# Transposing layer-norm rows on VectorE in 32x32 blocks, placed by DMA, instead of on TensorE

## The chip, the cores and the metric

The kernel runs on one NeuronCore of a Trainium2 chip. A core has engines with an instruction stream each: TensorE (PE in the profile, with PEld for its weight loads), VectorE (DVE), ScalarE (ACT), GpSimd (POOL) and SyncE (SP, which here only issues DMAs). They work side by side and wait for each other by semaphores; each takes its own instructions in order. The DMAs run on 16 DMA engines. Data lies in SBUF (128 partitions); TensorE writes to PSUM. The metric is the device time of one execution in microseconds. The kernel before takes 3035.59 us, the median of three runs (3035.33 to 3039.14).

## The reference

Two layers follow each other on x, 4 sequences of 1024 rows with 512 features, all in 32-bit floats.

```python
# layer 0: graph attention over 20 key rows, 16 heads, two directions
self_feat = concat([v, q_exp]) @ W_self.T + b_self
output = self_feat + gat(direction 0) + gat(direction 1)
x = v + relu(output)
# layer 1: a transformer block modulated by the condition c
sh_msa, sc_msa, g_msa, sh_mlp, sc_mlp, g_mlp = split(silu(c) @ W_mod + b_mod, 6)
x = x + g_msa * attention(layernorm(x) * (1 + sc_msa) + sh_msa, W_qkv, W_out, b_out)
x = x + g_mlp * (gelu((layernorm(x) * (1 + sc_mlp) + sh_mlp) @ W1 + b1) @ W2 + b2)
```

Attention has 16 heads of 64 features over 1024 keys; W1 is 512x2048 and W2 2048x512. The change concerns the two modulated layer norms, whose results stand in front of W_qkv and W1.

## The kernel before

Rows are taken in tiles of 128 (32 tiles, 8 for each sequence, called batch here), and for layer 1 in blocks of four tiles (VB = 4, 512 rows). Three stages follow each other.

**Graph attention** (up to about 412 us). A loop over s runs the 32 row tiles through a software pipeline: TensorE multiplies, DVE, ACT and POOL share the softmax. Its end writes x1 to DRAM and takes the row statistics. In its steps 14 to 27 the first two norm blocks (batch 0) are prepared.

**Attention** (412 to about 2270 us). There are 256 steps: 4 batches, 8 pairs of heads, 8 tiles of queries. In a step TensorE makes the scores of two heads ("psc"), DVE takes the row maxima ("mx"), ACT the exponentials ("w"), ACT and POOL scale them, and DVE transposes them in 32x32 blocks into "wd" (`turn`, L1191). Every second step SP issues eight DMAs that place these blocks in "wT" (L1195), and some two steps later TensorE multiplies them with the values ("pav"). "wd" has three buffers, "wT" two. All else is a list named `fill` of pieces with an earliest and a latest step, a cost in units and a place within the step: projections ("q"), output products ("pu"), loads, sums. A small planner chooses the steps of the products by unit costs; pieces with equal earliest and latest step stay where they are put. Place 4 is the end of a step. TensorE works in seven products instead of eight where blocks of 2x2 are multiplied (`seven`, L520), which needs sums of rows and of weights, made by POOL (`row_sum`, L610).

**MLP** (2270 us to the end). For each of 8 norm blocks, four groups of up products (seven each), then a down projection of seven products "a, c, b, a2, b2, d, b3" (32 matmuls each). The function `between` (L1637) stands after the first down product and prepares the next block; DVE and ACT are lightly loaded. One tile hT holds the normed rows for all blocks of the stage, so it can be written only when the up products are done.

**The norm.** `norm_load` (L412) fetches four row tiles into "xl" (SP). `norm_row` (L418) subtracts the mean and scales, in place. `norm_T` (L433) then makes hT, the transposed rows, 128 features on the partitions by 512 rows, for feature group c of four: four TensorE transposes into one PSUM bank, and one instruction of ACT (or DVE) that moves the bank to hT with the features' scale and shift:

```python
for n in range(VB):
    nc.tensor.transpose(
        pt[:, n * P : (n + 1) * P], xl[st, k * VB + n][:, c * P : (c + 1) * P], ident
    )
...
    nc.scalar.activation(hT[st, k][:, c, :], pt, AF.Identity, scale=scale, bias=shift)
```

Where these stand: in the graph-attention stage one c in each of the steps 17 to 20 and 24 to 27. In the attention stage, before the next batch begins at step `at`, two c in each of the steps at-12, at-11 and at-7, at-6 (L1267 to L1274); the row sums follow at at-7 to at-4 and the first products that read them from at-5. For the first MLP block, steps NS-11 and NS-10, with NS the number of steps (L1328). In the MLP stage all four c stand in `between`, where TensorE's banks "ma" and "mc" are used in turn, and for all blocks but the first every second c goes through DVE.

Of the kernel before, what the change touches and what calls it, by code (L numbers as in the profile page):

```python
# [15 lines left out]
ALU = mybir.AluOpType  # L16
# [25 lines left out]
def cond_block_kernel(  # L42
# [89 lines left out]
    with ExitStack() as gctx:  # L132
# [297 lines left out]
            for i in range(k * VB, (k + 1) * VB):  # L430
                norm_row(st, i, on_act)

        def norm_T(st, k, c, bank, on_act=True):  # L433

            sh, sc = NORM[st][4:]
            b = k * VB // NT
            if st == 1 and k > 0:
                hT[st, k] = hT[st, 0]
            elif c == 0:
                hT[st, k] = rp.tile([P, FC, VB * P], F32, name="hT", tag="hT", bufs=2)  # L440
            pt = bank("ptn")
            for n in range(VB):
                nc.tensor.transpose(
                    pt[:, n * P : (n + 1) * P], xl[st, k * VB + n][:, c * P : (c + 1) * P], ident
                )
            scale, shift = modT[:, sc + c, b : b + 1], modT[:, sh + c, b : b + 1]
            if on_act:
                nc.scalar.activation(hT[st, k][:, c, :], pt, AF.Identity, scale=scale, bias=shift)  # L448
            else:
                nc.vector.tensor_scalar(hT[st, k][:, c, :], pt, scale, shift, ALU.mult, ALU.add)  # L450

        def load_w(held, key, tag, src, cols):

# [176 lines left out]
        def mlp_rows():  # L630

            h = hT[1, 0]
            if "mlp" not in tx:
                tx["mlp"] = xp.tile([P, 6, F], F32, name="tx", tag="tx")
            o = [tx["mlp"][:, k, :].rearrange("p (c r) -> p c r", c=2) for k in range(3)]
            sums_b(nc.gpsimd, o, h[:, :2, :HB], h[:, :2, HB:], h[:, 2:, :HB], h[:, 2:, HB:])
# [221 lines left out]
            if 0 <= i < NTA:  # L858
                f(i)

        def bank_l0(name):
            return ps.tile([P, F], F32, name=name, tag="tr")

        def bank_pf(name):
            return psa.tile([P, F], F32, name=name, tag="pf", bufs=2)

# [7 lines left out]
        for s in range(-4, NTA + 2):  # L874
            do(g_load, s + 4)
            if s >= -2:
                do(g_loadmask, s + 4)
            if s in (1, 7, 13, 23):
                g_modload(s // 6)
            do(g_scores, s)  # L880
            if s == 1:

                do(g_self, s + 2)
            if s == NTA:
                ahead(4)
# [24 lines left out]

            if s in (6, 12, 22, 29):
                g_mod((s - 5) // 6 - s // 29)
            if s == 12:
                rstd(rs1, mv1, nm1, 0, NT)
            if s in (14, 21):
                norm_load(0, s // 7 - 2)
            if 15 <= s - s // 22 * 7 <= 16:
                for i in range(2):
                    norm_row(0, s // 22 * VB + 2 * ((s - 15) % 7) + i)
            if s in (17, 18, 19, 20, 24, 25, 26, 27):  # L920
                norm_T(0, s // 24, (s - 17) % 7, bank_l0)
# [19 lines left out]
    with ExitStack() as actx:  # L941
# [9 lines left out]
        NB = S // QB  # L951
        wout, gate = {}, {}
        vt, oT, xr, wn, wd, wT = {}, {}, {}, {}, {}, {}

        turns = []

        def bank_q(name):

            turns.append(0)
            return (q1, q2)[len(turns) % 2]  # L960


        def load_out(b, g):

# [258 lines left out]
        def add(lo, hi, units, place, f, *args):  # L1223
            fill.append((lo, hi, units, place, lambda: f(*args)))
# [15 lines left out]
        for b in range(B):  # L1240
# [22 lines left out]
            for gp in range(NP):  # L1263
                g, p = divmod(gp, 2)
                at = s0 + gp * NT
                if gp == 0 and b > 0:
                    for h, (ld, rws, tr) in enumerate(  # L1267
                        ((-18, (-15, -14, -14, -13), -12), (-10, (-9, -9, -8, -8), -7))
                    ):
# [279 lines left out]
    with ExitStack() as mctx:  # L1549
# [42 lines left out]
        def new_bank(name):  # L1592

            flip.append(0)
            return up_banks[("ma", "mc")[len(flip) % 2]]

        def short():
            return mp2.tile([P, F], F32, name="s", tag="s", bufs=2)

        flip = []  # L1600
        rows2 = {}
        NB2 = NTA // VB
        for k in range(NB2):
# [32 lines left out]

            def between():  # L1637
                if nxt < NB2:
                    for c in range(FC):
                        norm_T(1, nxt, c, new_bank, on_act=(k == 0 or c % 2 == 1))  # L1640
                if k * VB % NT == 0:
                    spread(2, b, gate2)
                    spread(3, b, bias2)
                for n in range(VB):
                    i = k * VB + n
                    rows2[n] = rp.tile([P, F], F32, name="x2", tag="xl", bufs=VB)
                    nc.sync.dma_start(rows2[n], x2d[i])
                if nxt < NB2:
                    mlp_rows()
# [73 lines left out]
```

## Time and profile before

One execution was taken by the profiler: its span from the first to the last instruction is 3034.2 us, 1.4 us less than the median of the three runs (3035.59); a time of its own for that execution, outside the span, is not given.

| what | value |
|---|---|
| median of three runs | 3035.59 us |
| span of the profiled execution | 3034.2 us |
| PE busy in the span | 2999.3 us (99%) |
| DVE / ACT / POOL busy | 1999.6 / 1432.0 / 1339.4 us |
| attention stage, 412 to 2270 us: PE / DVE busy, DMA share | 1842.62 / 1485.13 us, 0.75 |
| MLP stage, 2270 to 3034 us: PE / DVE / ACT busy, DMA share | 755.90 / 213.27 / 159.53 us, 0.11 |
| norm transposes on PE | 256 of 128x128, 0.272 us each, overlapping |
| modulation from PSUM, ACT / DVE | 0.777 / 0.810 us each |
| granted TensorE clock | 1.000 |

Busy time of PE counts overlapping matmuls once and its ends are modelled, so a PE that is busy for 99% is not necessarily what every step waits for; the chain of waits and the gaps between products tell more. The DMA share is the mean busy share of the 16 DMA engines. A row of the group views gives line, engine, operation, output and input tile, count, and the duration as minimum, median and maximum in ns.

### The profile page before, as it was taken

Reading aid. Unit: us, or ns where it says so; the run is one execution under the profiler, and the core shown is the slowest. Engines: PE = TensorE matmul, PEld = TensorE weight load, DVE = VectorE, ACT = ScalarE, POOL = GpSimd, SP = SyncE. Lnnn points to the kernel's source line nnn. Section 1 sums busy time; section 2 is a strip of 40 time slices with the busy share of each in tenths; the row PEclk is TensorE's granted clock in tenths of the full one; section 3 lists DMA queues with packets and bytes.
Section 4 is the critical chain, followed back from the end, with each engine's and each line's share of the span. In section 5 each row is a group of like instructions: output and inputs, shape, how many; then the busy total and the mean of one; then the engine's idle time right before and its main releaser. Section 6 shows DMA issues by size and latency. Waiting matters only on the chain.

```text
span 3034.2 us, 41780 instructions
## 1 busy us (share of the span) xinstructions
PE 2999.3 (99%) x15317; PEld 1980.2 (65%) x15317; DVE 1999.6 (66%) x2836; ACT 1432.0 (47%) x2368; POOL 1339.4 (44%) x922
## 2 busy tenths in 40 slices
PE   9999999999999999999999999999999999999999
PEld 6666655555555555555555555555568888888888
DVE  3888867777878877878787878877863222222322
ACT  3344456555755565755555755556641221112211
POOL 1444456555656655656655656655721110111010
PEclk9999999999999999999999999999999999999999
DMA  6433357777868777768777868766871010101110
GB/s 201 140 118 121 117 129 180 162 171 179 192 157 210 181 168 179 192 155 211 187 159 180 191 159 205 189 162 164 203 196 63 14 49 28 49 21 35 35 42 15
DMA packets 282695, 417.90 MB, mean 138 GB/s; under 512 B 28968, under 2 KB 101092, under 8 KB 282492
## 3 DMA queue, kind: packets, MB, share of 16 engines
q1 hardware_dynamic: 282256, 415.03, 53.8%
q8 instruction: 123, 2.02, 0.3%
q14 instruction: 80, 0.66, 0.1%
q10 hardware_dynamic: 236, 0.20, 0.0%
HBM read 120.93 MB, written 25.76 MB: 48 GB/s over the span
## 4 chain that ended last, share of the span: by engine, by line
PE 83%; DVE 7%; ACT 3%; POOL 3%; issue 2%; DMA 2%; SPq 1%; POOLq 0%; DVEq 0%; ACTq 0%
PE q L533 19%; PE psc L1156 15%; PE pav L1064 13%; PE pu L1139 6%; PE mbd L533 5%; PE mbu L533 5%; PE mad L533 4%; PE mau L533 3%; PE mcd L533 2%; PE mdd L533 2%; PE mdu L533 2%; PE mcu L533 2%; DVE mx L1167 1%; ACT w L1173 1%; POOL t L742 1%
## 5 line engine op out<-in xcount | busy, mean ns | idle before, releaser
L1182 POOL TENSOR_SCALAR w<-w,sm 128x1024 f32<-128x1024 f32 x256 | 728.6, 2846 | 701.5 <-DVE sm L1178 686.4
L1173 ACT ACTIVATE w<-psc,mx 128x1024 f32<-128x1024 f32 x512 | 570.7, 1115 | 642.6 <-DVE mx L1167 641.6
L1191 DVE STREAM_TRANSPOSE wd<-w 128x1024 f32<-128x1024 f32 x512 | 632.2, 1235 | 109.3 <-ACT w L1180 96.0
L1167 DVE TENSOR_REDUCE mx<-psc 128x1 f32<-128x1024 f32 x512 | 599.2, 1211 | 80.2 <-PE psc L1156 77.0
L1156 PE MATMUL psc<-kT,qT 64*128 64x512 f32 x2048 | 526.9, 615 | 3.1 <-ACT kT L1024 1.4
L1064 PE MATMUL pav<-wT,v 128*64 128x256 f32 x4096 | 482.1, 383 | 1.2 <-DMA wT<-wd 0.6
L1064 PEld LDWEIGHTS pav<-wT,v 128*64 128x64 f32 x4096 | 296.1, 137 | 224.0 <-issue 86.0
L1156 PEld LDWEIGHTS psc<-kT,qT 64*128 64x128 f32 x2048 | 201.6, 186 | 220.5 <-issue 151.2
L1180 ACT ACTIVATE w<-w,sm 128x1024 f32<-128x1024 f32 x256 | 291.0, 1137 | 0.0
L512 POOL TENSOR_TENSOR tx<-hT 128x512 f32<-128x512 f32 x8 | 10.3, 1288 | 596.5 <-ACT hT L448 596.5
L1148 DVE TENSOR_TENSOR xr<-pu,xr 128x512 f32<-128x512 f32 x210 | 143.5, 683 | 78.9 <-PE pu L1139 78.7
L533 PE MATMUL q<-hT,wqk 128*128 128x512 f32 (+1 forms) x396 | 181.2, 581 | 1.0 <-DVE q L547 1.0
L555 ACT COPY mbu<-mau 128x512 f32<-128x512 f32 x30 | 17.1, 570 | 276.5 <-PE mau L533 276.5
L719 PE MATMUL pa<-kp,sfT 128*128 128x320 f32 x512 | 143.5, 433 | 1.4 <-ACT sfT L694 1.4
L533 PEld LDWEIGHTS q<-hT,wqk 128*128 128x128 f32 x396 | 74.7, 190 | 80.9 <-issue 78.2
L533 PE MATMUL q<-tx,ex 128*128 128x512 f32 (+1 forms) x264 | 123.5, 591 | 1.8 <-POOL tx L618 1.3
L719 PEld LDWEIGHTS pa<-kp,sfT 128*128 128x128 f32 x512 | 94.8, 190 | 38.2 <-ACT sfT L694 1.9
L679 PE MATMUL pf<-wx,xT 128*128 128x512 f32 x256 | 116.0, 596 | 0.0
L533 PE MATMUL mad<-w,hs 128*128 128x256 f32 x512 | 113.1, 379 | 0.0
L533 PEld LDWEIGHTS mad<-w,hs 128*128 128x128 f32 x512 | 97.3, 190 | 13.2
L1139 PE MATMUL pu<-wout,oT 128*128 128x256 f32 x360 | 98.4, 396 | 4.2 <-DVE xr L1148 3.7
L1139 PEld LDWEIGHTS pu<-wout,oT 128*128 128x128 f32 x360 | 62.6, 189 | 59.3 <-issue 31.6
(309 smaller groups left out, 4590.7 us busy)
## 6 DMA issues: line engine op xcount, KB each, us to landing
wT<-wd SPq DMA_DIRECT2D x1024, 256.0 KB
wqk<-in_w_qkv SPq DMA_DIRECT2D x64, 256.0 KB
xT<-in_xt SPq DMA_DIRECT2D x32, 256.0 KB
xs<-in_x SPq DMA_DIRECT2D x32, 256.0 KB
x1d<-xs SPq DMA_DIRECT2D x32, 256.0 KB
xl<-x1d SPq DMA_DIRECT2D x32, 256.0 KB
wv<-in_w_qkv SPq DMA_DIRECT2D x32, 256.0 KB
xr<-x1d SPq DMA_DIRECT2D x32, 256.0 KB
```

Of the source, the lines that this page charges most:

```text
L533: nc.tensor.matmul(t[:, q * width : (q + 1) * width], lhsT=lhs(which, q, k), rhs=rhs(which, q, k), start=(fresh and q == 0 and k == 0), st ...
L679: nc.tensor.matmul(pfs[i], lhsT=xT[i][:, c, :], rhs=wx[:, c, :], start=False, stop=(c == FC - 1), skip_group_check=True,)
L719: nc.tensor.matmul(pas[i][:, n, :HF], lhsT=sfT2[i][:, c, :], rhs=kp[:, b, c, n * HF : (n + 1) * HF], start=False, stop=(c == FC - 1), skip ...
L1064: nc.tensor.matmul(po[j * D : (j + 1) * D, :], lhsT=vt[b, g][:, m, p * P + j * D : p * P + (j + 1) * D], rhs=w[:, j, :, m, :], start=(m == 0),
L1139: nc.tensor.matmul(pu[0][:, q * HB : (q + 1) * HB], lhsT=a[:, q * P : (q + 1) * P], rhs=r, start=(bool(fresh) and q == 0), stop=True, skip ...
L1148: nc.vector.tensor_tensor(o, pu[0].rearrange("p (r f) -> p r f", r=2), o, ALU.add)
L1156: nc.tensor.matmul(sc[j][:, n * F : (n + 1) * F], lhsT=qT[b, gp][q, t * P : (t + 1) * P], rhs=kT[b, gp][q, n * F : (n + 1) * F], start=Tru ...
L1167: nc.vector.tensor_reduce(mx, sc, axis=AX.X, op=ALU.max, negate=True)
L1173: nc.scalar.activation(w, sc, AF.Exp, bias=mx, accum_out=sm)
L1180: nc.scalar.mul(w, w, sm)
L1182: nc.gpsimd.tensor_scalar(w, w, sm, None, ALU.mult)
L1191: nc.vector.transpose(wd[j][:, :, at, :], wn.pop((b, gp, t, j)).rearrange("p (m k) -> p m k", k=U))
```

## The change

DVE now transposes each normed row tile in 32x32 blocks into a spare tile. In such a result a block stands still and only its inside is turned, so four DMAs on SP's queue for each row tile move the blocks to hT, in runs of 32 elements (128 B). A partition of hT then holds other features than before; the host puts the rows of W_qkv and W1, and the columns of W_mod and b_mod for shift and scale, into the same order. ACT applies scale and shift in place on hT.

```diff
+        def norm_turn(st, k, n, home):
+            if st == 1 and k > 0:
+                hT[st, k] = hT[st, 0]
+            elif n == 0:
+                hT[st, k] = rp.tile([P, FC, VB * P], F32, name="hT", tag="hT", bufs=2)
+            t = home(n)
+            nc.vector.transpose(
+                t.rearrange("p (m k) -> p m k", k=RB),
+                xl.pop((st, k * VB + n)).rearrange("p (m k) -> p m k", k=RB),
+            )
+            for u in range(P // RB):
+                at = n * P + u * RB
+                nc.sync.dma_start(hT[st, k][:, :, at : at + RB], t[RB * u : RB * (u + 1), :])
+
+        def norm_mod(st, k, c):
...
+            o = hT[st, k][:, c, :]
...
+            nc.scalar.activation(o, o, AF.Identity, scale=scale, bias=shift)
+
+        def home_blocks(key):
+            def home(n):
+                if key not in blocks:
+                    blocks[key] = xp.tile([P, 6, F], F32, name="tt", tag="tx")
+                return blocks[key][:, n, :]
...
-            if s in (17, 18, 19, 20, 24, 25, 26, 27):
-                norm_T(0, s // 24, (s - 17) % 7, bank_l0)
+            if s in (17, 18, 24, 25):
+                for i in range(2):
+                    norm_turn(0, s // 24, 2 * ((s - 17) % 7) + i, home_blocks(0))
+            if s in (19, 20, 26, 27):
+                for i in range(2):
+                    norm_mod(0, s // 24, 2 * ((s - 19) % 7) + i)
...
-                        ((-18, (-15, -14, -14, -13), -12), (-10, (-9, -9, -8, -8), -7))
+                        ((-18, (-15, -14, -14, -13), (-12, -12, -11, -11), -10), (-10, (-9, -9, -8, -8), (-8, -8, -7, -7), -6))
...
+                        for n, tn in enumerate(tr):
+                            add(at + tn, at + tn, 0, 4, norm_turn, 0, 2 * b + h, n, home_blocks(b))
                         for c in range(FC):
-                            add(at + tr + c // 2, at + tr + c // 2, 0.4, 3, norm_T, 0, 2 * b + h, c, bank_q)
+                            add(at + md, at + md, 0, 4, norm_mod, 0, 2 * b + h, c)
                     for k in range(4):
-                        add(at - 7 + k, at - 7 + k, 0, 4, row_sum, b, k)
+                        add(at - 6 + k, at - 6 + k, 0, 4, row_sum, b, k)
...
+        for n in range(VB):
+            add(NS - 11 + n // 2, NS - 11 + n // 2, 0, 4, norm_turn, 1, 0, n, home_blocks("mlp"))
         for c in range(FC):
-            add(NS - 11 + c // 2, NS - 11 + c // 2, 0.4, 3, norm_T, 1, 0, c, bank_q)
+            add(NS - 9, NS - 9, 0, 4, norm_mod, 1, 0, c)
...
             def between():
                 if nxt < NB2:
-                    for c in range(FC):
-                        norm_T(1, nxt, c, new_bank, on_act=(k == 0 or c % 2 == 1))
+                    for n in range(VB):
+                        norm_turn(1, nxt, n, lambda n: short() if n % 2 else tx["mlp"][:, 5, :])
...
+            def modulated():
+                for c in range(FC):
+                    norm_mod(1, nxt, c)
+                mlp_rows()
...
                 if n == 0:
                     between()
+                if n == 3 and nxt < NB2:
+                    modulated()
```

The tile "tt" takes the place of the row sums "tx" in SBUF before these are made. The transposed rows of a block now stand two tiles to a step in the steps where TensorE's transposes stood or one step earlier, all four modulations of a block in one later step (at-10, at-6, NS-9), and the row sums at at-6 to at-3. In the MLP stage the transposes and their DMAs stand in `between`, with two spare places (the last sixth of "tx" for even tiles and the short buffers for odd ones); modulation and row sums follow after the fourth down product.

More of the change, by code (lines that the diff above doesn't have):

```diff
@@ L431, in norm_rows @@
                 norm_row(st, i, on_act)
-        def norm_T(st, k, c, bank, on_act=True):
+        RB = 32
+        blocks = {}
+        def norm_turn(st, k, n, home):
[12 more added lines that the diff above has]
+        def norm_mod(st, k, c):
             sh, sc = NORM[st][4:]
             b = k * VB // NT
[L437 to L445, printed above, removed]
-            scale, shift = modT[:, sc + c, b : b + 1], modT[:, sh + c, b : b + 1]
[L447 to L450, printed above, removed]
+            o = hT[st, k][:, c, :]
+            scale, shift = modT[:, sc + c, b : b + 1], modT[:, sh + c, b : b + 1]
+            nc.scalar.activation(o, o, AF.Identity, scale=scale, bias=shift)
[4 more added lines that the diff above has]
+                return blocks[key][:, n, :]
+            return home
         def load_w(held, key, tag, src, cols):
@@ L859, in do @@
                 f(i)
-        def bank_l0(name):
-            return ps.tile([P, F], F32, name=name, tag="tr")
         def bank_pf(name):
@@ L953, in cond_block_kernel @@
         vt, oT, xr, wn, wd, wT = {}, {}, {}, {}, {}, {}
[L955 to L960, printed above, removed]
         def load_out(b, g):
@@ L1266, in cond_block_kernel @@
                 if gp == 0 and b > 0:
-                    for h, (ld, rws, tr) in enumerate(
-                        ((-18, (-15, -14, -14, -13), -12), (-10, (-9, -9, -8, -8), -7))
+                    for h, (ld, rws, tr, md) in enumerate(
+                        ((-18, (-15, -14, -14, -13), (-12, -12, -11, -11), -10), (-10, (-9, -9, -8, -8), (-8, -8, -7, -7), -6))
                     ):
@@ L1590, in dn_rhs @@
             return w2s[2 * h + k][:, r, f * HB : (f + 1) * HB]
-        def new_bank(name):
-            flip.append(0)
-            return up_banks[("ma", "mc")[len(flip) % 2]]
         def short():
             return mp2.tile([P, F], F32, name="s", tag="s", bufs=2)
-        flip = []
         rows2 = {}
@@ L1647, in between @@
                     nc.sync.dma_start(rows2[n], x2d[i])
-                if nxt < NB2:
-                    mlp_rows()
                 for n in range(VB):
                     nc.gpsimd.tensor_tensor(rows2[n], rows2[n], bias2, ALU.add)
+            def modulated():
+                for c in range(FC):
+                    norm_mod(1, nxt, c)
+                mlp_rows()
             def dn_done(i, j, t):
@@ L1684, with spread_features @@
     mask = np.asarray(mask_BxSxSx11_ik0)
+    def spread_features(a):
+        n = f // P
+        return a.reshape(n, n, P // n, -1).transpose(1, 2, 0, 3).reshape(a.shape)
+    w_mod, b_mod = np.array(L1_cond_W_mod), np.array(L1_cond_b_mod)
+    for k in (0, 1, 3, 4):
+        cols = slice(k * f, (k + 1) * f)
+        w_mod[:, cols] = spread_features(w_mod[:, cols].T).T
+        b_mod[cols] = spread_features(b_mod[cols])
     adj = np.stack([mask[:, :, :NG, :], mask[:, :NG].transpose(0, 2, 1, 3)])
@@ L1701 @@
         "gbo": L0_cond_bout,
-        "w_mod": L1_cond_W_mod,
-        "b_mod": L1_cond_b_mod,
-        "w_qkv": L1_cond_W_qkv,
+        "w_mod": w_mod,
+        "b_mod": b_mod,
+        "w_qkv": spread_features(np.asarray(L1_cond_W_qkv)),
         "w_out": L1_cond_W_out,
         "b_out": L1_cond_b_out,
-        "w1": L1_cond_W1,
+        "w1": spread_features(np.asarray(L1_cond_W1)),
         "b1": L1_cond_b1,
```

## The prediction

> **What bounds the kernel now.** The page's first part gives PE 2999.3 of 3034.2 us, so I went to stages, then to the places where the change acts. The chain of waits names PE for 83% of the span, and it also shows where PE is not the bound.
>
> The MLP stage first: the timeline around the end of one product of the down projection (start, duration, engine, line, operation).
>
> ```profile
> 2385.76 7.07 PE L533 MATMUL mad<-w,hs 128*128 128x256 f32 x32
> 2392.45 0.57 PEld L443 LDWEIGHTS mcu<-ident,xl 128*128 128x128 f32 x4
> ...
> 2394.17 0.42 PEld L443 LDWEIGHTS mcu<-ident,xl 128*128 128x128 f32 x4 [0.70 <-DVE hT L450]
> ...
> 2394.66 0.63 PE L443 MATMUL mau<-ident,xl 128*128 128x128 f32 x4
> ...
> 2395.13 7.07 PE L533 MATMUL mcd<-w2x,hx 128*128 128x256 f32 x32
> ```
>
> Products follow each other every 6.91 us here except where the norm's sixteen transposes stand: the chain has "mad" from 2385.92 to 2392.83 and "mcd" from 2395.29, a gap of 2.46 us that PE alone pays.
>
> Then the attention stage at a change of batch, with engine time by windows (width, then busy time and count for PE, PEld, DVE, ACT, POOL, then clock, DMA share, GB/s). The old transposes stand at 780, 786, 811 and 817.
>
> ```profile
> 700.00:775.00 75.00, 74.65 (x423) 44.76 (x422) 58.31 (x76) 44.93 (x70) 44.91 (x32) 1.00 0.72 174
> 775.00:781.00 6.00, 6.00 (x38) 3.45 (x37) 5.76 (x8) 4.93 (x8) 2.85 (x1) 1.00 0.34 55
> 781.00:787.00 6.00, 6.00 (x41) 3.59 (x39) 5.53 (x8) 4.92 (x8) 2.85 (x1) 1.00 0.90 201
> 787.00:794.00 7.00, 6.92 (x36) 3.92 (x36) 6.50 (x11) 6.19 (x11) 3.15 (x2) 1.00 0.94 239
> 794.00:800.00 6.00, 5.90 (x34) 3.02 (x34) 5.93 (x8) 2.96 (x6) 5.34 (x5) 1.00 0.91 228
> 800.00:806.00 6.00, 5.81 (x33) 3.04 (x32) 5.39 (x9) 4.01 (x7) 2.84 (x1) 1.00 0.97 272
> 806.00:812.00 6.00, 6.00 (x36) 3.56 (x36) 5.62 (x8) 4.99 (x8) 2.85 (x1) 1.00 0.90 244
> 812.00:818.00 6.00, 6.00 (x39) 4.22 (x38) 5.71 (x8) 5.19 (x9) 5.19 (x3) 1.00 0.76 181
> ```
>
> Here three things are full at once: PE, DVE (40.4 of 43 us from 775 to 818) and the DMA engines (33.2 of the 37 us from 781 to 818). The chain of waits in the same place passes through a load:
>
> ```profile
> 796.90 1.19 PE pav L1064 x9
> 798.09 4.70 DMA xl<-x1d
> 802.79 0.02 issue
> 802.81 1.52 ACT xl L421 x2
> ```
>
> SP's own timeline there is back to back: eight "wT" DMAs from 789.61 for 8.37 us, four "xl" loads (798.09, 3.09 us), eight "wT" DMAs from 801.95 for 8.70 us, one "wout" load; the next pause is 811.3 to 814.75. The change adds DMAs and DVE work at this place.
>
> **The change part by part.** Prices come from these rows.
>
> ```profile
> L1191 DVE STREAM_TRANSPOSE wd<-w x512: 1203/1235/1248, 415.2 to 2232.9; 128x1024 f32<-128x1024 f32 x171
> L421 ACT ACTIVATE xl<-xl,nm,rs x28: 799/805/821, 760.6 to 2156.3; 128x512 f32<-128x512 f32 x28
> L363 SPq DMA_DIRECT2D vb<-vrd x36: 274/337/349, 42.8 to 58.4; - x36
> ```
>
> A norm row tile (128x512) becomes one DVE transpose, half the 1235 ns: 0.62 us; and four SP DMAs, each 64 KB in 512 runs of 128 B. There are 64 row tiles, so 256 new DMAs: 32 in the graph-attention stage, 96 at the three batch changes, 16 for the first MLP block, 112 in the MLP stage. Removed are 256 PE transposes. The modulation stays 64 instructions of 128x512, 12 of them moved from DVE to ACT in the MLP stage, where ACT is busy 160 of 764 us; in place one costs 0.805 (nearest row L421) where it cost 0.777: under 2 us in all, hidden by ACT's idle half.
>
> Price of one new DMA. No SBUF-to-SBUF transfer in 128 B runs exists before. The nearest row in run length is the spread of the "vb" values (128 B runs from DRAM): the DMA view of 56 to 58 us.
>
> ```profile
> q1 hardware_dynamic: 355, 0.04, 12.6%
> ```
>
> That is 0.126 x 16 x 2 us / 355 = 11.4 ns a packet; 32 packets on each of 16 engines give 0.36 us. From above: the "wqk" loads (512 B runs, 341 to 344 us: 1322 packets at 92.8%) take 34 ns a packet, some of them longer runs; the run of 512 such packets would be 1.1 us at most. Between them, "wT" (SBUF to SBUF) takes 1.05 us for 256 KB where the "xl" load takes 0.77: factor 1.36. I take 0.36 x 1.36 = 0.49 us, say 0.5, as the vb row is the nearest in run length; the ends are 0.36 and 1.1. SP's issue of 0.34 lies inside that. The Trainium skill (DMA: Bandwidth & Descriptors, Rules for kernel authors) warns against transposing by a plain DMA with a rearranged access pattern and puts the loss at 19 times. From wT's 0.26 us for 64 KB that would be an estimated 5 us a DMA, some 150 us a batch change, and a time near 3550; the vb row speaks against it, since here each run is 32 elements and not one. The same page (Why small descriptors are slow) says that SBUF-to-SBUF transfers are spared the penalty; then a DMA would be an estimated 0.26 us, the batch changes would cost only DVE's share below, and the sum would be near 3033. No run before shows either.
>
> MLP stage. Seven gaps close: 2.68 (the first, 2293.45 to 2296.13) + 6 x 2.46 = 17.4 us, all on PE. The cover is the down projection, 7 products x 6.91 = 48 us from the first one's start. Inside it must fit: transposes after DVE's sums end (2387.7, while PE is in the first product), the third waiting for the first one's DMAs since they share a slot, sixteen DMAs at 0.5 (8 us, 18 at the upper end) with about 1.6 us landing (798.09 + 4.70 against 3.09 of issue), the four "x" loads queued behind them on SP (2.6), ACT's four modulations (3.2), POOL's sums after its bias adds (8 x 1.27). In series about 27 us from the first product's start, 34 at the upper end. ACT's copy of the "c" product may wait for a short buffer; its reader on PE comes 14 us later. Only if the series passed 48 us would the next up product be late, so I take -17.4; the ends are that and -10, one us kept in each gap by the shared buffers.
>
> Graph-attention stage. PE loses 8 groups of four (weight loads 252.04 to 252.48: 0.43 each), 3.4 us; DVE gains 8 x 0.62 = 5.0, in four steps of about 10 us in which it is busy 8.6 and its softmax instructions carry the chain. Ends -3.4 and +5.0; I take +1, as PE is shown full (10.00 of 10) beside a DVE with 1.4 us free for 1.24 in each. DMA there is at a third.
>
> Attention stage, three batch changes and one MLP block. PE is relieved of 4.15 us a change, 2.08 for the block (windows of those instructions alone). That is worth nothing where DVE and DMA are full too, so 0; if PE alone were the bound, -14.5.
> DVE: 8 x 0.62 = 5.0 a change against 2.6 free. That is +2.4 a change alone, and it would overlap with the next.
> DMA: 32 x 0.5 = 16 us a change into 3.8 free. Behind them on SP wait the "wT" DMAs, for these "pav" on PE and the "wd" ring on DVE, then ACT, whose modulations stand in order before the next exponentials and now need all DMAs of their rows to have landed. The wT DMAs have some slack: issued 801.95 to 810.65, read two steps after their step began (about 814.3), with 1.6 to land: 2 us for PE, about 4 for DVE's ring. I take 3. So 16 - 3.8 - 3 = 9 a change; three are 27. For the MLP block 8 us into 2 free less the slack: 3. Sum +30. Ends: at 0.36 us 11.5 - 6.8 = 5, with a step (6) more of slack nothing, and DVE's 2.4 remains: +8; at 1.1 us 35 - 6.8 = 28 a change and 13: +97.
> Order: four modulations stand in one step (3.2 us) instead of two in each of two, and the row sums come one step (6.2) later while the products that read them keep their places. The first needs 2 x 0.8 + 2 x 1.27 = 4.1 us after ACT gets there, PE is back after about 2 us of scores: +2 a change, 6 in all; ends 0 and 15. Behind the waiting sum on POOL stands the next scaling of the weights (2.85 us), and POOL has some 3 us free in a step. The wait exists today in small ("PE q L533 <- POOL tx L618: 1.3, 2").
>
> Sum against the profiled span: 3034.2 - 17.4 + 1 + 30 + 6 = 3053.8; the median of the runs shown is 1.4 us above that span, so 3055.
>
> **The rivals.** *Queue hidden (faster)*. The new DMAs fit because wT's slack is a step larger than I read, or because packets cost 11 ns or less. For it: SP waits for DVE at L1195 498 us in total, so on average it has room. Against: the pauses are not in these windows. Then -17.4 + 1 + 8 + 0 gives 3027. It decides once a DMA costs under about 0.36 us, where the overflow is inside the slack. *Everything to PE (faster)*. DVE is no bound either and all 35 us of PE (17.4 + 3.4 + 14.5) come through: 3000. Against it, DVE's 40.4 of 43. *Packets dear (slower)*. 0.8 us a DMA: 25.6 - 6.8 = 19 a change, 8 for the block: +65, giving 3090; at 1.1 it is +97, 3122. For it: neither row has short runs on both the reading and the writing SBUF side. *The MLP gain fails*: the waits through the shared slot pass 48 us; +17 to any of these. It needs DMAs above 2 us (16 of them reach 32 us beside the 18 of the rest).
>
> **How the numbers follow.** Likeliest (queue partly in the way, 3036 to 3075): 0.5, forecast 3055. Packets dear (3075 to 3122): 0.17. MLP gain fails too: 0.02. Queue hidden: 0.23, mostly 3015 to 3034. Everything to PE: 0.08. A measurement of this kernel tells about 0.2% (6 us) from no change. Of the hidden queue 0.19 lies below 3029.5 and 0.04 in the band, and 0.03 of the likeliest does: faster 0.27, same 0.07, slower 0.66. The range 3015 to 3095 leaves out about 1 in 10 on each side; the likeliest's own range is 3036 to 3075.
>
> **What would show it.** Right: in the MLP stage products at 6.91 us without gap; around the batch changes DMA share near 1 over some 50 us, SP without pause, waits of "pav" or of DVE's "wd" on "wT", of ACT's modulation on the hT DMAs, and windows that are some 10 us longer; packets of 128 B near 15 ns. Wrong: a batch change as long as before with DMA below 0.95, or an MLP gap that remains before "mcd" or in front of the next up product.

## The result and the profile after

The changed kernel takes 3122.45 us (median of four runs, 3120.5 to 3125.46) against 3036.76 us before on the same chip (3035.33 to 3039.14): 1.0279 times as long, with a 95% interval from 1.0264 to 1.0294. The prediction was 3055 with a range from 3015 to 3095. The direction was right and the size was not: 86 us were lost where 19 were expected, and the time lies outside the range. The profiled execution has a span of 3123.7 us, 89.5 more than before, and a mean granted clock of 0.987 (1.000 before).

Where the 89.5 us lie can be read from where each stage begins, with the first scores as the mark of the attention stage: it begins 12.1 us later than before. Each of the three batch changes then adds 27.9, 25.3 and 25.5 us and the preparation of the first MLP block 15.9. The MLP stage is shorter, 747.0 us against 763.8. That makes 12.1 + 94.6 - 16.8 = 89.9, the span's difference but for reading errors.

The MLP stage, read as before from the timeline around the end of the first down product:

```profile
2392.98 7.07 PE L549 MATMUL mad<-w,hs 128*128 128x256 f32 x32
2399.88 7.07 PE L549 MATMUL mcd<-w2x,hx 128*128 128x256 f32 x32
```

The gap of 2.46 us in front of "mcd" is gone; products follow each other after 6.90 us, as the prediction had it.

A change of batch, by windows (columns as in the windows shown of before):

```profile
805.00:811.00 6.00, 4.92 (x24) 2.67 (x26) 5.93 (x9) 2.76 (x5) 3.57 (x2) 1.00 0.72 96
811.00:817.00 6.00, 2.19 (x14) 1.11 (x10) 1.11 (x2) 2.60 (x4) 2.10 (x3) 0.85 0.82 136
817.00:823.00 6.00, 4.53 (x9) 2.20 (x10) 3.02 (x5) 3.80 (x7) 1.47 (x1) 0.58 0.91 227
...
847.00:853.00 6.00, 0.03 (x2) 0.00 (x0) 2.36 (x2) 2.86 (x5) 5.10 (x6) 0.69 0.85 144
853.00:859.00 6.00, 4.86 (x6) 2.19 (x7) 2.60 (x4) 3.29 (x6) 2.61 (x2) 0.50 0.89 232
```

Before, PE was nearly full in each window here. Now it is busy for only 2.19 of 6 us at 811 to 817 and for 0.03 at 847 to 853, and DVE for 1.11 and 2.36. These are not full engines but waits that stop nearly everything. Behind each the granted clock is low for one window, 0.58 and 0.50. The timeline names what ended the waits (in brackets: idle time before the instruction, and its releaser):

```profile
814.40 2.92 ACT L457 ACTIVATE hT<-hT,modT 128x512 f32<-128x512 f32 x4 [6.63 <-DMA hT<-tt]
818.47 3.85 PE L1165 MATMUL psc<-kT,qT 64*128 64x512 f32 x7 [5.17 <-ACT w L1182]
...
850.14 2.93 ACT L457 ACTIVATE hT<-hT,modT 128x512 f32<-128x512 f32 x4 [4.54 <-DMA hT<-tt]
851.74 2.35 POOL L634 TENSOR_TENSOR tx<-hT 128x1024 f32<-128x1024 f32 x1 [0.82 <-ACT hT L457]
854.14 3.78 PE L549 MATMUL q<-tx,ex 128*128 128x512 f32 x4 [7.12 <-POOL tx L634]
```

In the first case ACT stands in front of its four modulations until the new DMAs have landed; the next exponentials are queued behind them, so DVE and then PE run dry. In the second the wait passes through the modulations to POOL's row sum and then to the first product that reads it. SP's timeline in the same stretch has no pause:

```profile
789.84 8.95 SPq L1204 DMA_DIRECT2D wT<-wd  x8
798.90 1.79 SPq L472 DMA_DIRECT2D wqk<-in_w_qkv  x2
800.80 11.68 SPq L449 DMA_DIRECT2D hT<-tt  x16
812.58 8.39 SPq L1204 DMA_DIRECT2D wT<-wd  x8
821.07 3.38 SPq L415 DMA_DIRECT2D xl<-x1d  x4
824.56 10.54 SPq L1204 DMA_DIRECT2D wT<-wd  x8
...
835.86 12.22 SPq L449 DMA_DIRECT2D hT<-tt  x16
```

The chain of waits there names the queue itself. From 810.39 to 826.91 it follows SP's issue instructions one after the other and goes on to a wT DMA and to DVE, where before it was PE that filled the chain:

```profile
812.58 0.57 SPq L1204
...
825.80 1.11 SPq L1204
...
826.96 4.54 DMA wT<-wd
831.52 1.29 DVE tt L443 x2
```

And the new instructions, from the group views of their lines (count, then minimum, median and maximum in ns):

```profile
L449 SPq DMA_DIRECT2D hT<-tt x144: 609/636/1717, 260.6 to 2277.4; - x144
L443 DVE STREAM_TRANSPOSE tt<-xl x36: 661/683/703, 259.9 to 2260.8; 128x512 f32<-128x512 f32 x36
L457 ACT ACTIVATE hT<-hT,modT x64: 797/799/815, 281.5 to 2990.9; 128x512 f32<-128x512 f32 x64
```

A DMA takes SP 0.64 us to issue (median); the two sixteens above take 11.68 and 12.22 us. Two causes were therefore open: the queue of DMAs, and the new order of row sums and products. In the expectations below, Q stands for the queue, O for the order of the pieces and V for VectorE's added work.

### The profile page after: what moved, and what is told of

It reads as the page before. It is cut to its first block, busy times and chain, and to the rows that moved or that the text cites. A ratio compares the mean times of both kernels' runs of the same rounds, so it can differ in the third digit from the quotient of the medians.

```text
span 3123.7 us, 41795 instructions
## 1 busy us (share of the span) xinstructions
PE 3008.3 (96%) x15061; PEld 1957.5 (63%) x15061; DVE 2035.1 (65%) x2888; ACT 1441.5 (46%) x2380; POOL 1341.0 (43%) x922
## 3 DMA queue, kind: packets, MB, share of 16 engines
q8 instruction: 121, 1.98, 0.3%
## 4 chain that ended last, share of the span: by engine, by line
PE 76%; DVE 8%; DMA 4%; POOL 3%; SPq 3%; issue 3%; ACT 2%; POOLq 0%; ACTq 0%; DVEq 0%
PE q L549 17%; PE psc L1165 14%; PE pav L1073 12%; PE pu L1148 6%; PE mbd L549 5%; PE mbu L549 5%; PE mad L549 4%; PE mau L549 3%; SPq L1204 2%; DVE mx L1176 2%; DMA wT<-wd 2%; PE mdd L549 2%; PE mcd L549 2%; PE mdu L549 2%; PE mcu L549 2%
## 5 line engine op out<-in xcount | busy, mean ns | idle before, releaser
L1165 PE MATMUL psc<-kT,qT 64*128 64x512 f32 x2048 | 546.2, 626 | 32.9 <-ACT w L1182 30.3
L1656 POOL TENSOR_TENSOR x<-x,tx 128x512 f32<-128x512 f32 x32 | 40.0, 1280 | 617.0 <-DMA x<-x2d 617.0
L1187 DVE RECIPROCAL sm<-sm 128x1 f32<-128x1 f32 x512 | 72.3, 141 | 74.3 <-ACT w L1182 51.7
```

Of the source, the lines that this page charges most:

```text
L1165: nc.tensor.matmul(sc[j][:, n * F : (n + 1) * F], lhsT=qT[b, gp][q, t * P : (t + 1) * P], rhs=kT[b, gp][q, n * F : (n + 1) * F], start=Tru ...
```

## The experiments

Apart from the first, each kernel has one time beside one or more of the kernel before. The changed kernel's own times spread over 5 us, so differences of that size are not read as gains or losses.

### The MLP part alone

The kernel before, with the change in the MLP stage only. At the batch changes TensorE still transposes. The first MLP block too, but ScalarE writes its normed rows with the features already in the new order.

```diff
+        def norm_row_spread(n):
+            t = home_blocks("mlp")(n)
+            nc.scalar.activation(
+                t.rearrange("r (c a b) -> r b c a", c=FC, b=FC),
+                xl[1, n].rearrange("r (b c a) -> r b c a", b=FC, c=FC),
...
-            add(NS - 15 + n, NS - 15 + n, 0, 4, norm_row, 1, n, True)
+            add(NS - 12 + n // 2, NS - 12 + n // 2, 0, 4, norm_row_spread, n)
-            add(NS - 11 + c // 2, NS - 11 + c // 2, 0.4, 3, norm_T, 1, 0, c, bank_q)
+            add(NS - 10 + c // 2, NS - 10 + c // 2, 0.4, 3, norm_T, 1, 0, c, bank_q)
```

> The change in the MLP stage alone; the graph-attention stage, the batch changes and the first MLP block keep TensorE's transposes (the first MLP block's rows are normed one to three steps later, out of place, so that the features come in the new order). All theories take the MLP stage's gain as independent of the rest: the stage was 763.8 us before and 747.0 after, so 3020 us, 0.994 of before, with 2 us of doubt for the first MLP block. If the loss at the batch changes had its root in the MLP stage's code, it would stay and the time would be above 3030.

Measured: 3020.41 us (median of four, 3019.73 to 3022.49) against 3038.38 before in the same comparison (seven runs, 3035.39 to 3048.14): ratio 0.9934, interval 0.9913 to 0.9955. That is a small gain, 0.7%, but clear of the noise, as expected, and it beats both kernels. The span is 3020.5 us, 13.7 less than before's; the attention stage ends 2.5 us later than there and the MLP stage is 16 us shorter.

```profile
2386.87 7.07 PE L578 MATMUL mad<-w,hs 128*128 128x256 f32 x32
2393.78 7.07 PE L578 MATMUL mcd<-w2x,hx 128*128 128x256 f32 x32
```

Here too "mcd" follows 6.91 us after "mad". So the gain of the MLP stage is real, and the whole loss lies in the two stages ahead of it.

### The DMAs alone, added to the kernel before

Nothing of the change is made; the kernel before issues the DMAs of the batch changes and of the first MLP block in addition, from a tile that is there into a spare one that nobody reads.

```diff
+        def more(key, n):
+            if key not in extra:
+                extra[key] = xp.tile([P, 6, F], F32, name="tt", tag="tx")
+            for u in range(4):
+                at = n * P + u * 32
+                o = extra[key][:, :FC, at : at + 32]
+                nc.sync.dma_start(o, gates[32 * u : 32 * (u + 1), :])
...
+                            e = (-12, -12, -11, -11)[n] if h == 0 else (-9, -9, -8, -8)[n]
+                            add(at + e, at + e, 0, 4, more, b, n)
...
+            add(NS - 11 + n // 2, NS - 11 + n // 2, 0, 4, more, "mlp", n)
```

> The kernel before, with the DMAs of the batch changes and of the first MLP block added and nothing else: 16 of 64 KB in 128 B runs a block, from a constant tile to a spare one, 112 in all, that nothing reads. Theory Q (the DMAs hold up SP's queue, and what stands behind them is late): the wT DMAs are some 10 us late at each change, +8 to +12 us for each of three and +4 for the block, 3065 to 3077. Theory A (the loss is ACT waiting for the landing of what it modulates, in front of its exponentials): nobody waits here, below +10, 3037 to 3047. Theory V (DVE and the later order): no change, 3037.

Measured: 3103.82 us, 65 more than before and above every expected range. Some 20.5, 18.6 and 17.5 us are lost at the three changes and 10 at the block. SP's timeline of this kernel at the first change, and its chief waits there (total us, times, longest):

```profile
789.93 11.14 SPq L461 DMA_DIRECT2D tt<-gates  x16
801.17 8.54 SPq L1206 DMA_DIRECT2D wT<-wd  x8
809.81 3.35 SPq L415 DMA_DIRECT2D xl<-x1d  x4
813.22 7.26 SPq L461 DMA_DIRECT2D tt<-gates  x8
...
830.52 6.41 SPq L461 DMA_DIRECT2D tt<-gates  x8
```

```profile
DVE wd L1202 <- DMA wT<-wd: 15.5, 3, 9.7
...
ACT xl L421 <- DMA xl<-x1d: 14.0, 2, 13.1
```

The DMAs take SP 11.1 + 7.3 + 6.4 = 24.8 us at a change. What waits is what stands behind them in the queue: ACT for its rows, DVE's ring for the wT DMAs. The queue alone can cost most of what the change costs, though nobody reads what these DMAs bring. Two differences from the change remain: the second block's DMAs stand one step earlier here, and the spare tile takes the place of the row sums, which waited 2.5 us for these DMAs in the whole run.

### Longer runs, and fewer DMAs

Two variants of the same addition: the same number and size with runs of 2 KB instead of 128 B, and a quarter of the number (28 of 256 KB) with runs of 128 B.

```diff
-                o = extra[key][:, :FC, at : at + 32]
+                o = extra[key][32 * u : 32 * (u + 1), n, :]
```

> As the kernel with added short runs, but each of the 112 DMAs writes its 64 KB in 32 runs of 2 KB. Theory Q with a price for each run: SP issues one in about 0.35 us instead of 0.63, some 3 us a change, 3040 to 3052. Theory Q with a price for each DMA or byte: as with short runs, 3065 to 3077. Theories A and V: no change, 3037.

```diff
-            for u in range(4):
...
+            o = extra[key].rearrange("p a f -> p (a f)")[:, 768 * n : 768 * n + 768]
+            nc.sync.dma_start(
+                o.rearrange("p (r k) -> p r k", k=48)[:, :, :32], gates.rearrange("p (r k) -> p r k", k=32)
+            )
```

> The same bytes in the same 128 B runs as the kernel with added short runs, but four DMAs of 256 KB (2048 runs) a block instead of sixteen of 64 KB. If SP's time is a price for each DMA: four times 0.63 us, little is late, 3037 to 3048. If it is a price for each run, in issue or in the DMA engines: four times 2.5 us, as with sixteen, 3065 to 3077.

Measured: 3100.98 us with long runs and 3094.14 us with wide DMAs, 63 and 56 more than before. The issue row of the three, in the order short, long, wide (one kernel each):

```profile
L461 SPq DMA_DIRECT2D tt<-gates x112: 623/639/1767, 789.9 to 2244.1; - x112
```

```profile
L461 SPq DMA_DIRECT2D tt<-gates x112: 507/588/1692, 789.4 to 2241.3; - x112
```

```profile
L459 SPq DMA_DIRECT2D tt<-gates x28: 633/1764/4861, 790.4 to 2229.0; - x28
```

Runs sixteen times as long shorten the issue only from 639 to 588 ns, so with 64 KB each the length of the runs is not what SP pays for. A quarter of the number was expected to cost little, and that was wrong: one of 256 KB takes 1764 ns where four take 4 x 639 = 2556. Here the DMA engines are full as well; their share for SP's queue over 788 to 806 us reads

```profile
q1 hardware_dynamic: 10314, 3.40, 102.7%
```

(packets, MB, share of 16 engines; it is 78.0% with the 64 KB DMAs and 67.5% with the long runs). The wT DMAs behind them get slower in turn, 10.12 us for eight where they took 8.54 beside the short ones. Neither shape takes the cost away.

### The change without its DMAs at the batch changes and the first MLP block

```diff
-            t = home(n)
+            change = k > 1 if st == 0 else k == 0
+            t = hT[st, k][:, n, :] if change else home(n)
...
-            for u in range(P // RB):
+            for u in range(0 if change else P // RB):
```

> The changed kernel, but at the three batch changes and for the first MLP block DVE's transposes write straight into hT and the 112 DMAs that place them are left out, so attention and the first MLP block work on wrongly placed rows; the order of modulation and row sums, the graph-attention stage and the rest of the MLP stage stay as changed. Theory Q (SP's queue is held up by these DMAs, and the rest follows from it): the batch changes lose only DVE's and the order's part, 2 to 5 us each instead of 27, so 3122 - 80 = 3036 to 3050. Theory V (DVE's 0.68 us a tile and the later modulation and row sums): most of the loss stays, above 3090.

Measured: 3077.40 us, span 3075.2, between the two theories. The attention stage now loses 48.8 us instead of 94.6, so the DMAs are worth 45.8 in the changed kernel: 10.7, 11.3 and 9.2 at the changes and 14.6 at the MLP block. The other 48.8 us are lost with no new DMA there, 17.2, 14.0 and 16.3 at the changes and 1.3 at the block. Neither cause has it all. POOL's timeline, and the product that waits:

```profile
833.18 2.84 POOL L1192 TENSOR_SCALAR w<-w,sm 128x1024 f32<-128x1024 f32 x1 [1.79 <-PE pu L1149]
835.99 0.73 POOL L529 TENSOR_TENSOR wsum<-wout 128x256 f32<-128x256 f32 x1
...
838.84 2.35 POOL L635 TENSOR_TENSOR tx<-hT 128x1024 f32<-128x1024 f32 x1
...
841.24 3.78 PE L550 MATMUL q<-tx,ex 128*128 128x512 f32 x4 [6.25 <-POOL tx L635]
```

PE waits 6.25 us for the first row sum. Ahead of that sum POOL has no idle time from 833.18 on: a scaling of the weights and four sums of output weights stand before it in its order.

### The order alone, on the kernel before

One line of the kernel before is changed, so that the row sums come one step later; its DMAs, transposes and engines stay as they are.

```diff
-                        add(at - 7 + k, at - 7 + k, 0, 4, row_sum, b, k)
+                        add(at - 6 + k, at - 6 + k, 0, 4, row_sum, b, k)
```

> The kernel before with one number changed: the row sums of each batch at at-6 to at-3 instead of at-7 to at-4, as the change has them. Theory O (with the sums one step later, POOL makes the first of them behind its weight scaling and the sums of the output weights, and TensorE's first product at at-5 waits for it, which alone costs some 9 us, and the second some 4): 25 to 45 us in all, 3062 to 3083. Rival: the wait comes from the four modulations in one step or from DVE's extra work, and not from the place of the sums: below 10 us, 3037 to 3047.

Measured: 3074.54 us against 3036.74, 38 more: 13.4, 13.1 and 12.0 at the three changes. Its products that wait (timeline, PE only):

```profile
825.74 3.37 PE L533 MATMUL q<-tx,ex 128*128 128x512 f32 x4 [3.42 <-POOL tx L618]
...
858.83 3.78 PE L533 MATMUL q<-tx,wqk 128*128 128x512 f32 x4 [5.03 <-POOL tx L618]
```

In the kernel before the same two instructions of the first case read

```profile
818.12 2.36 POOL L618 TENSOR_TENSOR tx<-hT 128x1024 f32<-128x1024 f32 x1
```

```profile
820.75 1.95 PE L533 MATMUL q<-tx,ex 128*128 128x512 f32 x4 [0.49 <-ACT hT L448]
```

The sum ended at 820.48 and the product began at 820.75: 0.27 us of slack. (The 0.49 us in brackets ends with ACT's move of hT, which happened to end later than the sum, at 820.61.) A sum that is made a step later must stop PE. There are two such places at each change: the products of place at-5 need the first sum, and those some three steps later the last one, which in the new order stands behind eight sums of weights on POOL. At the first change the scores fall back by 4.3 us at the first of these products and by 7.0 at the second; another 2 us are lost some 14 us ahead of the first and were not followed up. A part of it goes with the clock: the two products take 3.37 and 3.78 us, at granted clocks of 0.58 and 0.50, where they took 1.95 and 1.98 before. With no DMA and no DVE work added, the place of the sums alone costs 38 us.

### Can the order's loss be taken back?

The products are moved with the sums, one step later, once in the changed kernel and once in the one without DMAs.

```diff
-            ("qk", 0, -5, -5), ("v", 0, -1, 0), ("qk", 1, 2, 3), ("qk", 2, 6, 11), ("v", 1, 9, 16), ("qk", 3, 14, 19),
+            ("qk", 0, -4, -4), ("v", 0, -1, 0), ("qk", 1, 2, 4), ("qk", 2, 6, 11), ("v", 1, 9, 16), ("qk", 3, 14, 19),
```

> The changed kernel with the first products of each batch one step later too, at at-4 instead of at-5, so that the sums have their old lead again (the planner then also places some output products elsewhere). Theory O: 8 to 14 us a change come back, 3080 to 3100. Rival (the late DMA queue alone decides when the sums can be made): 0 to 4 us a change, 3110 to 3122.

> The kernel without the batch changes' DMAs (wrongly placed rows as there), with the first products one step later. What is left at the batch changes is DVE's extra work and the four modulations in one step. Theory O: 8 to 14 us a change below the 3077 of the one without DMAs, 3035 to 3053. Theory V (DVE): most of the 16 us a change stay, 3065 to 3077.

Measured: in the changed kernel 3122.44 us, nothing gained. Without the DMAs 3056.63, 21 less than the 3077.40 with the products in their old places. Two of these lie in the graph-attention stage, so some 6.5 a change come back, fewer than expected; what remains, read in the middle of each batch, is 11, 8 and 9 us a change. In the changed kernel the product no longer waits, but PE stops elsewhere, for exponentials that stand behind the modulations:

```profile
818.06 4.87 PE L1165 MATMUL psc<-kT,qT 64*128 64x512 f32 x8 [6.71 <-ACT w L1182]
```

So the two causes lie over one another: while the queue is late, a better order gains nothing, and alone they cost 38 and 65 us on the kernel before, where together, with DVE's work and the later modulations, they cost 94.6. The remainder of 8 to 11 us a change was not split further. It holds DVE's eight transposes (8 x 0.68 = 5.5 us a change into 2.6 free), the four modulations in one step, and shifts of other products that the planner made.

### Later modulations, another queue, a warm TensorE

Three variants of the changed kernel. The modulations of the first block two steps later:

```diff
-((-18, (-15, -14, -14, -13), (-12, -12, -11, -11), -10), (-10, (-9, -9, -8, -8), (-8, -8, -7, -7), -6))
+((-18, (-15, -14, -14, -13), (-12, -12, -11, -11), -8), (-10, (-9, -9, -8, -8), (-8, -8, -7, -7), -6))
```

> The changed kernel with the modulation of the first block of each batch change at at-8 instead of at-10, one line. Theory A (ACT waits for the hT DMAs in front of its exponentials, 6.6 us at the first change, and TensorE with it): that wait and the slow clock behind it go, 6 to 10 us a change, 3092 to 3104. Theory Q, with everything behind the late queue anyway: ACT will then wait for the late xl loads or DVE for wT instead, 0 to 3 us a change, 3113 to 3122.

The 112 DMAs of the batch changes and the first MLP block on POOL's queue instead of SP's:

```diff
+                e = nc.gpsimd if (k > 1 if st == 0 else k == 0) else nc.sync
+                e.dma_start(hT[st, k][:, :, at : at + RB], t[RB * u : RB * (u + 1), :])
```

> The changed kernel with the 112 DMAs of the batch changes and of the first MLP block issued by POOL instead of SP: the same bytes, runs and DMA engines. If the price is SP's issue and the place in SP's queue: wT is no longer behind them, 10 us or more a change come back, 3075 to 3095, unless POOL's own issue delays its scaling of the weights. If the price is the DMA engines' time: 3115 to 3130. POOL has some 3 us free in a step; if it needs more than 0.4 us for a DMA, it is slower than 3122.

Extra matmuls into a bank that nobody reads, to fill PE's waits:

```diff
+        def warm_up(n):
+            for _ in range(n):
+                nc.tensor.matmul(q1, lhsT=ident, rhs=gates, start=True, stop=True)
+        add(NS - 9, NS - 9, 0, 5, warm_up, 14)
+        for b in range(1, B):
+            at = b * NP * NT
+            add(at - 9, at - 9, 0, 5, warm_up, 12)
+            add(at - 5, at - 5, 0, 0.4, warm_up, 14)
```

> The changed kernel with matmuls that nobody reads put where TensorE waits: 12 of 128x512 (5.2 us) at the end of step at-9, 14 (6.0 us) ahead of the first product at at-5 and at the end of step NS-9. In the changed kernel the granted clock is at half for 82 us around the batch changes and the first MLP block. If the half clock costs time of its own, it goes to 1.0 there and 10 to 30 us come back: 3092 to 3112. If TensorE waits anyway while its clock is low, nothing comes back: 3117 to 3130, and more where a matmul that nobody reads delays the next scores.

Measured: 3120.39, 3143.12 and 3132.84 us, beside 3122.45 for the change as it is. Later modulations give back 2 us, which is within the spread: ACT no longer waits for the hT DMAs of the first block, but stops all the same for the rows that are loaded behind them:

```profile
ACT xl L421 <- DMA xl<-x1d: 12.5, 2, 11.7
```

On POOL's queue each DMA occupies POOL for 747 ns, and it becomes the engine that is late, both for the DMAs and for the row sums (waits of 775 to 880 us):

```profile
ACT hT L458 <- DMA hT<-tt: 22.3, 2, 11.6
...
PE q L550 <- POOL tx L635: 14.2, 1, 14.2
```

With PE kept busy the granted clock is 0.998 instead of 0.987 and the time 10 us longer. This does not settle what the half clock costs, because the added matmuls took more than was meant (PE's timeline at the first change):

```profile
809.67 10.46 PE L1345 MATMUL q<-gates,ident 128*128 128x512 f32 x24
...
844.47 12.28 PE L1345 MATMUL q<-gates,ident 128*128 128x512 f32 x28
```

Each is two instructions, so they hold PE for 10.46 and 12.28 us, twice the 5.2 and 6.0 that the expectation put down, and longer than the waits of 5 to 7 us that they were to fill. A gain by the full clock and a loss by real work that stands behind them can cover each other here. The kernel with the late sums shows that the half clock costs something: the two products behind its waits are 3.2 us longer together, of 13.4 lost at the first change.

### The graph-attention stage: six loads two steps later

In the change the last eight DMAs of this stage and six weight loads are issued in the step in which the next rows are loaded. Here the weight loads come two steps later.

```diff
-            if s == 25:
+            if s == 27:
                 load_qk(0, 0)
```

> The changed kernel with the six loads of the first attention weights issued two steps later in the graph-attention stage (s = 27 instead of 25), so that the loads of x in the next step no longer stand behind eight hT DMAs and these six. If ACT's wait for x, in front of its other work, makes the stage's loss of 9 to 12 us: the attention stage starts 4 us or less later than before, not 9 to 12, and the whole is 3110 to 3118. If DVE's transposes make it: no change, 3118 to 3124.

Measured: the attention stage begins 3.2 us later than before instead of 12.1 (8.4 to 11.3 in six other runs of the same code). The wait of ACT for its rows (330 to 420 us), in the change and then in this kernel:

```profile
ACT xs L175 <- DMA xs<-in_x: 9.2, 2, 7.5
```

```profile
ACT xs L175 <- DMA xs<-in_x: 3.1, 2, 1.9
```

So most of the loss of this stage was a load that stood behind others on SP. The time is 3118.53 us, and the span 6.9 us shorter than the change's (3116.8): the changes and the block read 27.3, 27.1, 26.6 and 15.8, together 2.2 more than there, which takes back a part of the 8.9.

## Why the prediction was wrong

| term | predicted, us | measured, us | from |
|---|---|---|---|
| MLP stage | -17.4 | -16.8 | stage times; -15.8 with the MLP part alone |
| graph-attention stage | +1 | +12.1 | start of the attention stage |
| DMAs and DVE at three changes | +27 | DMAs +31.2 | change against no DMAs |
| DMAs at the first MLP block | +3 | +14.6 | change against no DMAs |
| order at three changes | +6 | +47.5 with DVE's work; the sums' place alone +38 | no DMAs against before |
| the rest at the MLP block | 0 | +1.3 | no DMAs against before |
| sum | +19.6 | +89.9 | |

The split between DMAs and order depends on which is added first: on the kernel before, the DMAs of the changes alone cost 57 us and those of the block 10.

**The failed step is "Order".** It said "+2 a change, 6 in all; ends 0 and 15". The place of the sums alone costs 38, beyond its upper end. The step counted ACT's modulations and two row sums from the moment ACT gets there, and took PE to be busy with scores for about 2 us of that. It did not look at what else POOL had queued ahead of the sum, though it named the scaling that stands behind. And it took a small total of waiting ("1.3, 2") for slack: the sum ended 0.27 us before the product began. By the prediction's own figure a step is 6.2 us, and the sums were moved by one: most of a step had to be paid, and at two places of each change (4.3 and 7.0 us at the first change), where the step counted one of 2 us.

**The MLP term was right**, and so was its cover: 48 us of down products hid transposes, DMAs, modulations and sums.

**The DMA term at the changes, 31.2 for 27, was right in size by luck.** 0.5 us a DMA was taken from the time of the packets. The trace has 14.6 ns a packet, near the 15.5 worked out, but SP's issue is 0.64 us, nearly twice the 0.34 of the "vb" row (DMAs of 10 KB at most), which was put inside the 0.5. With the 24.8 us that the issue takes at a change, the same formula gives 24.8 - 3.8 - 3 = 18, and the DMAs alone on the kernel before cost 17.5 to 20.5, twice the 9 that was forecast. In the changed kernel they add only 9 to 11, because they and the order's waits cover each other in part. The Trainium skill (DMA: Bandwidth & Descriptors) gave two estimates: 5 us a DMA by the 19 times of its Rules for kernel authors, and 0.26 by Why small descriptors are slow, which spares such transfers. Neither fits this case: the packets of a DMA take 0.47 us on 16 engines and its issue 0.64. The 19 times compares with the hardware's DMA transpose, which no run here has. The same page (Issuing engines are not separate DMA queues) calls the time to initiate a DMA usually small beside the DMA itself; in these runs it is more than the time of the packets, 0.64 against 32 x 14.6 ns = 0.47.

**The MLP block's DMA term was mis-sized**, 14.6 for 3. The prediction let eight us flow into what is free. In the trace the second half of the DMAs is issued only after eight wT DMAs and two loads:

```profile
2255.40 5.78 SPq L449 DMA_DIRECT2D hT<-tt  x8
2261.28 8.52 SPq L1204 DMA_DIRECT2D wT<-wd  x8
2269.84 2.61 SPq L472 DMA_DIRECT2D wv<-in_w  x2
2272.55 5.49 SPq L449 DMA_DIRECT2D hT<-tt  x8
```

and ACT waits for them in one piece:

```profile
ACT hT L457 <- DMA hT<-tt: 12.5, 1, 12.5
```

It was not tried whether another step would spare this.

**The graph-attention term was mis-sized**, 12.1 for 1: it weighed PE against DVE and looked at the DMA share (a third), but not at the order on SP, where one late load of rows holds up the pipeline's end. With six loads moved, 3.2 us of it are left.

Of the rivals, "packets dear" named the time (3090 to 3122) but not the cause: packets cost what was forecast, and the issue and the order made up the rest. "Queue hidden" fell with the first added DMAs, "everything to PE" with the result itself, and "the MLP gain fails" with the stage's 16.8 us. Of the signs named in advance, SP without a pause and ACT waiting for the hT DMAs came true; DMA share near 1 did not (0.69 to 0.95 from 805 to 859 us), since SP's issue and not the engines was the limit.

## What to carry to other kernels

Before moving a producer by a step, read in the trace when its result is ready and when its first reader starts: where these touch, the price can be the whole step, at each place that reads, and a short total of waiting is no slack. Price a DMA on a busy queue by its issue time, taken from a row of the same size and shape, and follow what stands behind it. Before a filler is used to test a wait, check in its trace that it takes no longer than the wait. Where a change serves two stages with different limits, try it in the stage that has room: the MLP part alone is the version that beats both kernels.

## What the runs showed of the hardware

- A DMA of 64 KB whose source has 32 partitions takes SP 0.61 us or more to issue back to back with runs of 128 B and 0.51 or more with runs of 2 KB (medians 0.64 and 0.59); one of 256 KB in runs of 128 B had a median of 1.76. The stores to "x1d" and the "vb" loads took 0.33 and 0.34 us. The length of the runs mattered little here; a quarter of the number still took SP 16.2 us of the 24.8 at the first change.
- The same DMA issued by POOL takes 0.747 us of POOL's own time and lands 6.8 us after its issue (median).
- In the changed kernel the granted clock was at half for 82 us ahead of the kernel's end, in twelve pieces of 3.4, 6.8 or 10.2 us; the kernel before has none until its last microsecond. The Trainium skill (TensorE: Matmul & The Clock Gate, Part 1: The HAM clock gate) has half speed after an idle window of some 3.4 us. That agrees in the main: at the first change two pieces follow PE's waits of 5.17 and 7.12 us; but a third follows a wait of only 2.9 (at 883 us). Filling the waits with matmuls brought the clock back (0.998) but no time, with fillers longer than the waits.
